# A drain of GpSimd behind the second last scatter of a sparse graph-attention kernel

## The chip, the cores and the metric

The kernel runs on one NeuronCore of a Trainium2 chip. The metric is device time in microseconds (us); the time shown is the median of three runs. Beside it stands one profiled execution, taken by the hardware profiler, from which all durations below come.

## The reference

One graph-attention layer over 3327 nodes with 1024 features, after a layer norm and a ReLU:

```python
h = jnp.maximum(_layernorm(x, axis=-1), 0.0)
f = h @ Wf + bf
g = h @ Wg + bg
e = jax.nn.relu(f @ g.T)
scores = jnp.where(adj > 0, e, NEG)          # NEG = -9e15
attention = jax.nn.softmax(scores, axis=1)
out = x + attention @ (h @ W + bW)
```

`adj` is symmetric with ones on its diagonal and holds about 0.5% ones, so that a node has some 10 to 40 neighbours.

## The kernel before

The kernel uses the sparsity. Its first part (up to about 265 us) normalises the rows into a table `hd` in device memory, multiplies Wf and Wg into one matrix, and turns the rows of `adj` into neighbour lists `pd`, sorted by degree. Its second part handles the nodes in 26 tiles of 128 (`NT` is 26). For each tile t it gathers neighbour rows of `hd` with indirect DMAs that GpSimd issues (`gather`, recorded at line 639), takes dot products with the tile's queries (VectorE, L1260), forms the softmax (ScalarE), adds up the weighted rows (VectorE L1313, ScalarE L1296 and TensorE L1300), and multiplies the sum by W (TensorE, L1328).

The end of a tile is a chain. `rc` scales the product from PSUM into a result buffer `xp`, of which there are two (`res`, used in turn): on ScalarE, L1339, for all tiles but the last, and on VectorE, L1337, with x added, for the last. For all tiles but the last `X` then gathers the tile's rows of x on top of `xp`, as an adding DMA (line 639). Last comes `scatter`, an indirect DMA of GpSimd that writes the 128 rows of `xp` to their places in `out` (L1346).

The order of work on each engine is written out by a planner in Python: `planned` simulates the steps with their durations and gives each a start, and the loop

```python
for start, (op, *at), held in plan:
    ...
    made[op](*at)
```

issues them in that order. The order on each engine is then fixed; semaphores do the rest. On GpSimd the last steps are the gather of x for tile 24 (`X`), the scatter of tile 24, and the scatter of tile 25, one after the other with nothing between.

After the loop all five engines load a flag, `bad` (L1372), that says whether the graph fits the assumptions of the sparse path. If it doesn't, a dense path runs (L1384, `with tc.If(bad > 0)`); with this input it doesn't run. On the side where it doesn't, GpSimd has waits on the semaphores of its DMAs and then one instruction, INC_SWDGE_SEM[...]. The program ends at the close of the tile context (L1409): each engine executes a DRAIN and they meet at a barrier, of which GpSimd is the leader. SyncE first passes through a row of waits on the semaphores of the program, among them the eight that INC_SWDGE_SEM raises. A second, short barrier follows.

Of the kernel before, what the change touches and what calls it, by code (L numbers as in the profile page):

```python
# [579 lines left out]
def edge_path(ctx: ExitStack, tc: tile.TileContext, x, adj, Wf, bf, Wg, bg, W, bW, out, flag):  # L580
# [11 lines left out]
    nc = tc.nc  # L592
# [7 lines left out]
    NT = (N + P - 1) // P  # L600
# [567 lines left out]
    with tc.manual_schedule(engines={  # L1168
# [175 lines left out]
        def scatter(t):  # L1344
            whole = ORDER[t] < N // P
            ins = nc.gpsimd.indirect_dma_start(  # L1346
                out=out[:, :],
                out_offset=bass.IndirectOffsetOnAxis(
                    ap=perm[:, ORDER[t] : ORDER[t] + 1] if whole else final, axis=0
                ),  # L1350
                in_=res[t % 2],
                in_offset=None,
                bounds_check=None if whole else N - 1,
                oob_is_err=whole,
            )
            tc.declare_no_dep(ins.ins, group="results", reason="other rows")
            tc.add_to_no_dep_group("results", ins.ins)

        def told(_):
            nc.vector.tensor_copy(flag[0:1, 0:1], ps_y[1][0:1, 0, 0:1])  # L1360

        made = {
            "fl": told, "L": L, "H": H, "x": fetch_x, "C": C, "F": F, "G": fetch, "M": M, "hT": turned, "hc": hc, "q": third, "qc": qc,
            "fq": fq, "d": dot, "S": greatest, "A": A, "E": E, "Y": Y, "T": T, "w": w, "p": p, "s": s, "fo": fo, "yt": yt,
            "yc": yc, "W": project, "rc": rc, "X": X, "O": scatter,
        }
        plan = sorted(planned(ROWS, PASSES, SEED, WIDE)[1], key=lambda step: step[0])
# [8 lines left out]
def kernel(tc: tile.TileContext, x, adj, Wf, bf, Wg, bg, W, bW, out):  # L1376

    nc = tc.nc  # L1380
    with tc.tile_pool(name="flag", bufs=1) as fpool:
        flag = fpool.tile([1, 1], I32, name="flag")
        bad = edge_path(tc, x, adj, Wf, bf, Wg, bg, W, bW, out, flag)
        with tc.If(bad > 0):  # L1384
            dense_path(tc, x, adj, Wf, bf, Wg, bg, W, bW, out)
# [27 lines left out]
```

## Time and profile before

| what | us |
|---|---|
| median of three runs (lowest, highest) | 1232.57 (1228.5, 1233.57) |
| the profiled execution's own time | 1233.38 |
| its span, first to last instruction | 1231.6 |
| what lies around the span | 1.8 |
| PE busy in the span | 1099.2 (89%) |
| DVE busy | 1120.3 (91%) |
| POOL (GpSimd) busy | 936.7 (76%) |
| ACT busy | 602.7 (49%) |
| start of the scatter of tile 24, and of tile 25 | 1208.89, 1219.76 |

PE is TensorE, DVE is VectorE, ACT is ScalarE, POOL is GpSimd, SP is SyncE; a name with a q behind it is the engine's sequencer, which executes semaphore, branch and drain instructions. These are not counted as busy time. An arrow to the left in a row stands between what is written and what is read or, behind an idle time, before what ended it. Start times count from the beginning of the span.

### The profile page before, as it was taken

Reading aid. Unit: us, or ns where it says so; the run is one execution under the profiler, and the core shown is the slowest. Engines: PE = TensorE matmul, PEld = TensorE weight load, DVE = VectorE, ACT = ScalarE, POOL = GpSimd, SP = SyncE. Lnnn points to the kernel's source line nnn. Section 1 sums busy time; section 2 is a strip of 40 time slices with the busy share of each in tenths; the row PEclk is TensorE's granted clock in tenths of the full one; section 3 lists DMA queues with packets and bytes.
Section 4 is the critical chain, followed back from the end, with each engine's and each line's share of the span. In section 5 each row is a group of like instructions: output and inputs, shape, how many; then the busy total and the mean of one; then the engine's idle time right before and its main releaser. Section 6 shows DMA issues by size and latency. Waiting matters only on the chain. (4 is left out here: it accounts for less than half of the span.)

```text
span 1231.6 us, 14006 instructions
## 1 busy us (share of the span) xinstructions
PE 1099.2 (89%) x4508; PEld 697.5 (57%) x4508; DVE 1120.3 (91%) x2192; ACT 602.7 (49%) x924; POOL 936.7 (76%) x677
## 2 busy tenths in 40 slices
PE   2799990799939899999999999999899999999995
PEld 2566660466627466556655666665465656556553
DVE  5999998758898999998999999999999999999991
ACT  6899986324617355436452455443343333434240
POOL 8999996177676888878878778777887888787821
PEclk9899995799979999999999999999999999999998
DMA  9999999589788999989899899888998999998942
GB/s 370 420 396 397 393 359 324 191 313 350 270 257 281 329 314 315 319 285 339 302 342 308 307 306 320 279 286 299 317 294 288 311 310 321 283 316 256 324 118 54
DMA packets 101913, 374.43 MB, mean 304 GB/s; under 512 B 14859, under 2 KB 18602, under 8 KB 98631
## 3 DMA queue, kind: packets, MB, share of 16 engines
q0 software_dynamic: 79584, 286.77, 69.4%
q1 hardware_dynamic: 22246, 86.68, 18.7%
q8 instruction: 37, 0.61, 0.2%
q14 instruction: 46, 0.38, 0.1%
HBM read 344.11 MB, written 29.30 MB: 303 GB/s over the span
## 5 line engine op out<-in xcount | busy, mean ns | idle before, releaser
L639 POOL DMA_INDIRECT G<-hd,ps x454 | 567.4, 1250 | 159.2 <-issue 107.0
L1260 DVE CUSTOM_DVE_ANT_0 junk<-G,q 128x1024 bf16<-128x1024 f32 x468 | 563.9, 1224 | 34.0 <-DMA G<-hd,ps 19.2
L1328 PE MATMUL p_o<-W_sb,yT 128*128 128x512 f32 x832 | 365.8, 593 | 4.7 <-issue 3.1
L1313 DVE SCALAR_TENSOR_TENSOR G<-G,sc 128x1024 f32<-128x1024 f32 (+1 forms) x281 | 354.5, 1262 | 6.8 <-ACT G L1285 3.7
L1247 PE MATMUL p_q<-A_sb,hT 128*128 128x342 f32 x1152 | 350.5, 455 | 7.8 <-ACT p_q L1256 5.7
L1247 PEld LDWEIGHTS p_q<-A_sb,hT 128*128 128x128 f32 x1152 | 214.7, 191 | 116.4 <-issue 12.7
L1328 PEld LDWEIGHTS p_o<-W_sb,yT 128*128 128x128 f32 x832 | 155.1, 189 | 189.0 <-issue 180.9
L1300 PE MATMUL p_y<-ident,G 128*128 128x128 f32 x1552 | 190.1, 275 | 12.7 <-DVE G L1313 6.8
L1300 PEld LDWEIGHTS p_y<-ident,G 128*128 128x128 f32 x1552 | 175.0, 142 | 40.8 <-issue 15.3
L704 POOL TENSOR_TENSOR r<-r,iotaj 128x1664 f32<-128x1664 f32 (+3 forms) x50 | 183.9, 3750 | 3.9 <-ACT r L697 3.9
L1296 ACT ACTIVATE G<-G,sc 128x1024 f32<-128x1024 f32 x168 | 179.2, 1138 | 0.1
L837 PE MATMUL ps_A<-WgT,WfT 128*128 128x342 f32 x432 | 130.5, 461 | 1.6 <-ACT WfT L832 1.6
L767 DVE MAX8 cand<-r 128x8 f32<-128x208 f32 (+2 forms) x416 | 118.9, 360 | 4.0 <-POOL r L704 3.7
L1339 ACT ACTIVATE xp<-p_o,rs 128x512 f32<-128x512 f32 x50 | 34.2, 685 | 172.7 <-PE p_o L1328 131.5
L837 PEld LDWEIGHTS ps_A<-WgT,WfT 128*128 128x128 f32 x432 | 81.7, 193 | 42.1 <-issue 2.3
L697 ACT ACTIVATE r<-r 128x3327 f32<-128x3327 int32 (+3 forms) x27 | 77.3, 2865 | 10.2 <-DMA r<-in_adj_dram 10.2
L1253 ACT COPY q<-p_q 128x342 f32<-128x342 f32 x72 | 31.6, 443 | 103.0 <-PE p_q L1247 59.5
L1324 ACT COPY yT<-p_y 128x512 f32<-128x512 f32 x52 | 30.0, 587 | 71.6 <-PE p_y L1300 59.6
L1243 ACT COPY hT<-p_t 128x512 f32<-128x512 f32 x48 | 27.4, 585 | 74.4 <-PE p_t L1240 37.9
L639 POOL DMA_INDIRECT xp<-in_x_dram,perm x25 | 44.3, 1772 | 21.1 <-ACT xp L1339 14.4
L1281 ACT ACTIVATE sc<-sc,nm 128x10 f32<-128x10 f32 (+10 forms) x36 | 10.9, 304 | 94.4 <-DVE nm L1271 66.2
L1346 POOL DMA_INDIRECT out_dram<-xp,perm x25 | 32.8, 1310 | 31.1 <-DMA xp<-in_x_dram,perm 22.9
(148 smaller groups left out, 728.4 us busy)
## 6 DMA issues: line engine op xcount, KB each, us to landing
r<-in_adj_dram SPq DMA_DIRECT2D x24, 1663.5 KB, 12.8
xt<-in_x_dram SPq DMA_DIRECT2D x22, 512.0 KB, 13.6
hd<-xt SPq DMA_DIRECT2D x22, 512.0 KB, 10.5
G<-hd,ps POOLq DMA_INDIRECT x454
A_sb<-in_L_gnn_Wg_dram SPq DMA_DIRECT2D x8, 512.0 KB, 18.4
A_sb<-in_L_gnn_Wf_dram SPq DMA_DIRECT2D x8, 512.0 KB, 12.0
W_sb<-in_L_gnn_W_dram SPq DMA_DIRECT2D x8, 512.0 KB, 7.4
cd<-cand SPq DMA_DIRECT2D x25, 64.0 KB, 12.6
```

The lines of the kernel that those rows point to most:

```text
L639: return nc.gpsimd.indirect_dma_start(out=to, out_offset=None, in_=table, in_offset=bass.IndirectOffsetOnAxis(ap=idx, axis=0), **kw,)
L697: nc.scalar.activation(r[:n, b:e], a[:n, b:e], AF.Sign, accum_out=to)
L704: eng.tensor_mul(r[:n, b:e], r[:n, b:e], iotaj[:n, b:e])
L767: nc.vector.max(cands[t][:n, s * 8 : s * 8 + 8], r[:n, s * SW : min(N, (s + 1) * SW)])
L837: nc.tensor.matmul(ps[:, :QB], WfTs[c][:, k, :], WgT[:, k, o : o + QB], start=(k == 0), stop=(k == KD - 1))
L1247: nc.tensor.matmul(ps_q[(3 * t + i) % 2][:, :QB], hT[:, k, :], A_sb[:, k, i * QB : (i + 1) * QB], start=False, stop=(k == KD - 1), skip_gr ...
L1260: nc.vector.tensor_tensor_reduce(junks[k % 2], row(t, k), q[:, :D], 1.0, 0.0, op0=ALU.mult, op1=ALU.add, accum_out=scs[t % 3][:, k : k + 1],)
L1296: nc.scalar.activation(g, g, AF.Copy, scale=scs[t % 3][:, k : k + 1])
L1300: nc.tensor.matmul(ps_y[g][:, c, :], of[:, (4 * g + c) * P : (4 * g + c + 1) * P], ident, is_transpose=True, start=((t, g) not in begun an ...
L1313: nc.vector.scalar_tensor_tensor(y, row_k, scs[t % 3][:, k : k + 1], y, op0=ALU.mult, op1=ALU.add)
L1328: nc.tensor.matmul(ps_o[o], yT[:, k, :], W_sb[:, k, o * CB : (o + 1) * CB], start=False, stop=(k == KD - 1), skip_group_check=True,)
L1339: nc.scalar.activation(to, ps_o[o], AF.Copy, scale=rss[t % 3])
```

## The change

Behind the scatter of tile 24, the second last that GpSimd issues, a drain of GpSimd is written:

```diff
             )
             tc.declare_no_dep(ins.ins, group="results", reason="other rows")
             tc.add_to_no_dep_group("results", ins.ins)
+            if t == NT - 2:
+                nc.gpsimd.drain()
```

In the built program GpSimd has one DRAIN more, which waits for no semaphore and raises none. It stands between the scatter of tile 24 and the setting of a register for the scatter of tile 25. The instructions of all engines and their waits are otherwise the same, in the same order. Later source lines move down by two (L1372, L1384 and L1409 become L1374, L1386 and L1411).

## Prediction

> **What bounds the kernel now.** VectorE (91%) and TensorE (89%) bound the middle; the change touches neither, so I went to the end. First view, the chain that ended last, its last pieces (start, us, what):
>
> ```profile
> 1204.69 14.02 PE p_o L1328 x32
> 1218.70 0.02 issue
> 1218.72 0.76 DVE xp L1337
> 1219.49 0.03 issue
> 1219.52 0.51 POOLq L1372
> 1220.03 0.75 POOL out_dram L1346
> ```
>
> The last product ends at 1218.7, VectorE takes 0.76, and GpSimd scatters. The chain stops at 1220.8, yet the span lasts to 1231.6: 10.8 us hold no busy engine and are not in this view. Second view, the timeline of GpSimd from 1200 on (start, us; idle before in brackets):
>
> ```profile
> 1201.95 1.56 POOL L639 DMA_INDIRECT xp<-in_x_dram,perm  x1 [11.01 <-ACT xp L1339]
> 1208.89 0.98 POOL L1346 DMA_INDIRECT out_dram<-xp,perm  x1 [5.39 <-DMA xp<-in_x_dram,perm]
> 1219.76 1.02 POOL L1346 DMA_INDIRECT out_dram<-xp,final  x1 [9.88 <-DVE xp L1337]
> ```
>
> Between its last two scatters GpSimd idles 9.88 us, waiting for VectorE. The new drain stands there. Third view, the sequencers' instructions by line (durations in ns: least, median, most; then first and last start). L1384 is the branch, L1409 the end, L1401 the start of the program:
>
> ```profile
> L1384 POOLq EVENT_SEMAPHORE  x5: 17/43/43, 1223.0 to 1223.6; - x5
> L1384 POOLq INC_SWDGE_SEM  x1: 1533/1533/1533, 1223.6 to 1223.6; - x1
> ...
> L1409 SPq EVENT_SEMAPHORE  x12: 27/28/28, 1225.1 to 1225.8; - x12
> L1409 SPq DRAIN  x2: 7/7/7, 1225.9 to 1225.9; - x2
> L1409 POOLq DRAIN  x1: 5503/5503/5503, 1225.2 to 1225.2; - x1
> ...
> L1409 POOLq DRAIN  x2: 46/74/103, 1230.9 to 1231.3; - x2
> ...
> L1401 POOLq INC_SWDGE_SEM  x1: 27/27/27, 0.2 to 0.2; - x1
> L1401 POOLq DRAIN  x1: 169/169/169, 0.4 to 0.4; - x1
> ```
>
> So the end is: the last scatter lands (GpSimd's last wait for DMA ends at 1223.6), INC_SWDGE_SEM 1.53 us, then a DRAIN of 5.50 us that all others wait for. The same two instructions took 0.03 and 0.17 us at the start, before GpSimd had issued a DMA; between the start and the end it issues 576. A drain right behind the long one takes 0.10. Fourth view, busy time by stretch (PE, PEld, DVE, ACT, POOL, clock, DMA share, GB/s):
>
> ```profile
> 1209.90:1219.50 9.60, 8.79 (x21) 3.58 (x19) 1.50 (x2) 0.00 (x0) 0.00 (x0) 1.00 0.15 59
> 1225.20:1230.70 5.50, 0.00 (x0) 0.00 (x0) 0.00 (x0) 0.00 (x0) 0.00 (x0) 0.50 0.00 0
> ```
>
> During the 5.50 us no engine works and no DMA moves a byte: the drain isn't waiting for data under way.
>
> **The drain that is added.** It costs GpSimd's sequencer a time D in the idle stretch. The trace has two rows for D: 0.05 to 0.17 us where no DMA of GpSimd went before, 5.50 where hundreds did. Hundreds did here (all but one of 576), so I take 5.5. It starts once the scatter of tile 24 is issued (1208.9 to 1209.9); if it also waits for that scatter to land, from about 1212.6 (the scatter's last semaphore count in the trace). It ends between 1208.9 + 5.5 = 1214.4 and 1212.6 + 5.5 = 1218.1. Queued behind it are a register move, a semaphore wait of 17 ns, the last scatter with the DMA it issues, and the load of the flag; the scatter waits for VectorE until 1219.5. Nobody else waits for anything behind the drain, and GpSimd has no gather left to issue. Hidden by the last product, with 1.4 to 5.1 us to spare: cost 0. Without that cover it would be the whole 5.5.
>
> **What it takes from the end.** [...]
>
> INC_SWDGE_SEM: at least 0.03 (the start's row, which is another use of it), at most 1.53. In the trace it posts its eight semaphores 8 to 9 ns apart, the first 1.42 us after it begins; [...] I take 0.2 us. Saved 1.53 - 0.20 = 1.33; ends: 0 to 1.50.
>
> The DRAIN: 5.50 becomes about 0.2 (between the rows of 0.10 and 0.17 and a little more for one DMA). What is late next is SyncE, not GpSimd: its first wait is released by INC_SWDGE_SEM's posts (1225.1), twelve waits and two drains take it to 1225.93, and the barrier then opens in about 0.05. Before, GpSimd was at the barrier at 1230.77, 5.59 after INC_SWDGE_SEM's end at 1225.18; after the change the barrier comes 0.80 after that end. Saved 5.59 - 0.80 = 4.79, not 5.3.
>
> Sum: 4.79 + 1.33 = 6.1 us. The profiled execution would go from 1233.38 to 1227.3, its span from 1231.6 to 1225.5. That execution was 0.8 above the median of the runs shown; taken off the median, 1232.57 - 6.1 = **1226.5 us**. The other edits (nothing else changes in the program) cost 0.
>
> [...] The row: nothing in flight, a drain of 5.50. [...] the row shows a drain that took 5.50 with GpSimd's last record over at 1220.8 and its DMA landed by 1223.6, so something besides being idle is waited for; I go by the row. [...] while INC_SWDGE_SEM stayed at 1.53: sum 1232.57 - 4.79 = 1227.8. [...]
>
> **The rivals.** (a) The price comes back: the 5.50 belongs to whatever stands right before the last drain (the last scatter, or INC_SWDGE_SEM itself), or the new drain is a matter of 0.1 us that clears nothing. Then the end keeps its 10.8 us: 1232.6. For it: one long drain is all there is in the trace, so a fixed price for each drain after a DMA fits as well. Against it: INC_SWDGE_SEM, 57 times longer than at the start, shows a second instruction that has grown, and the short last drains show that one drain clears it. (b) Only the drain shrinks: 1227.8, as above. (c) Slower: the new drain outlasts its cover. The last scatter starts later once the drain takes over 9.6 us from 1209.9 (7.0 if it begins at the landing, 1212.6). To be slower than before it must overrun by more than what the end saves, so D beyond 9.6 + 6.1 = 15.7 us, or beyond 9.6 if rival (a) holds too; over 0.5% slower then needs D = 15.8. It would take a drain of nearly three times the one row there is, in a stretch in which TensorE and the DMAs are at work (DMA share 0.15). At D = 17 with nothing saved: 1232.6 + 7.4 = 1240.
>
> **How the numbers follow.** The bound of 0.5%, about what a measurement of this kernel can tell from no change, is 6.16 us, so 1226.4. Chances: [...] 0.82 (its own range: 1226.1 with INC_SWDGE_SEM at 0, and about 3 us either way for runs, whose three times spread over 5.1); (b) 0.04; (a) 0.10; (c) 0.04. The likeliest case stands almost on the bound: 6.1 against 6.16. What I have left uncounted goes one way ([...] the branch and the two short drains after the barrier come sooner or shorter), so I give two thirds of it, 0.55, to faster by over 0.5%, and 0.27 to within. Faster 0.55; within 0.27 + 0.04 + 0.10 = 0.41; slower 0.04. The range, 1222.5 to 1231.0, holds the likeliest case but for its edges (0.05) and all of (b), and leaves out (a) and (c): 0.81.
>
> **What the profile of the changed kernel would show.** A DRAIN of GpSimd at the scatter's line between 1209 and 1218, of about 5.5 us; the start of the last scatter still 0.3 behind VectorE's last record, at about 1219.8; INC_SWDGE_SEM at 0.2 to 0.3; the first drain of the end under 0.3; SyncE's drain, not GpSimd's, last before the barrier; some 4.7 us from the end of the last scatter to the end of the span in place of 10.8. The prediction is wrong if the last drain is still 5 us long (rival a), if INC_SWDGE_SEM keeps 1.5 (rival b), or if the last scatter's idle time is ended by GpSimd itself (rival c).

## The result, and the profile after

The changed kernel takes 1226.6 us (median of 22 runs, 1220.87 to 1233.30), the kernel before 1232.08 (median of 22 runs, 1221.88 to 1237.24). The ratio is 0.9959, with a 95% interval of 0.9942 to 0.9976: 0.4% faster, between 3.0 and 7.1 us. The profiled execution took 1224.52 us, with a span of 1222.7.

The end of the span is where to look. The sequencers' instructions by line, of the changed kernel (durations in ns: least, median, most; then first and last start). L1359 is the new drain, L1386 the branch and L1411 the end of the program, up to the barrier:

```profile
L1359 POOLq DRAIN  x1: 6652/6652/6652, 1205.8 to 1205.8; - x1
...
L1386 POOLq INC_SWDGE_SEM  x1: 203/203/203, 1220.9 to 1220.9; - x1
...
L1411 SPq EVENT_SEMAPHORE  x12: 27/28/28, 1221.1 to 1221.7; - x12
L1411 SPq DRAIN  x2: 7/7/7, 1221.8 to 1221.9; - x2
L1411 POOLq EVENT_SEMAPHORE  x2: 17/17/17, 1221.9 to 1222.0; - x2
L1411 POOLq DRAIN  x1: 140/140/140, 1221.2 to 1221.2; - x1
```

INC_SWDGE_SEM went from 1533 to 203 ns and the first drain of the end from 5503 to 140. GpSimd's drain is over at 1221.3; SyncE's second drain at 1221.9 is now the last before the barrier. The timeline of GpSimd, of the changed kernel:

```profile
1199.31 1.56 POOL L639 DMA_INDIRECT xp<-in_x_dram,perm  x1 [10.94 <-ACT xp L1339]
1206.06 0.99 POOL L1346 DMA_INDIRECT out_dram<-xp,perm  x1 [5.18 <-DMA xp<-in_x_dram,perm]
1217.12 1.02 POOL L1346 DMA_INDIRECT out_dram<-xp,final  x1 [10.08 <-DVE xp L1337]
```

The last scatter's wait is still ended by VectorE. The drain begins in the sequencer 0.24 us before the scatter of tile 24, whose issue is over at 1207.04, and goes on until 1212.47. What follows it on GpSimd, by line:

```profile
L1346 POOLq MOVE  x1: 29/29/29, 1212.5 to 1212.5; - x1
L1346 POOLq EVENT_SEMAPHORE  x1: 17/17/17, 1212.6 to 1212.6; - x1
L1346 POOL DMA_INDIRECT out_dram<-xp,final x1: 1017/1017/1017, 1217.1 to 1217.1; - x1
```

From the drain's end to VectorE's result at 1216.84 there are 4.4 us to spare. From the start of the last scatter to the end of the span it was 11.81 us before (1219.756 to 1231.562) and is 5.58 (1217.120 to 1222.695): 6.23 us less. The two profiled spans differ by 8.9; the other 2.6 us lie ahead of the last scatter, where the kernels are the same, and are within what runs of one kernel differ by (1220.87 to 1233.30 for the changed one).

### The profile page after: what moved, and what is told of

It is laid out like the page before. It is cut to its first block, busy times and chain, and to the rows that moved or that the text cites. A ratio compares the mean times of both kernels' runs of the same rounds, so it can differ in the third digit from the quotient of the medians.

```text
span 1222.7 us, 14007 instructions
## 1 busy us (share of the span) xinstructions
PE 1099.3 (90%) x4508; PEld 696.8 (57%) x4508; DVE 1121.7 (92%) x2192; ACT 601.9 (49%) x924; POOL 942.3 (77%) x677
## 5 line engine op out<-in xcount | busy, mean ns | idle before, releaser
L639 POOL DMA_INDIRECT G<-hd,ps x454 | 577.4, 1272 | 153.9 <-issue 98.2
L1240 PE MATMUL p_t<-ident,G 128*128 128x128 f32 x192 | 30.1, 286 | 27.9 <-DMA G<-hd,perm 27.7
```

The costliest lines, as they stand in the source:

```text
L639: return nc.gpsimd.indirect_dma_start(out=to, out_offset=None, in_=table, in_offset=bass.IndirectOffsetOnAxis(ap=idx, axis=0), **kw,)
```

## The experiments

They ran in two sets, each on one chip. The kernel before took 1242.54 us in the first (23 runs; the drains behind tiles 12, 16, 19 and 25) and 1240.18 in the second (31 runs; the others); times are compared within a set, and kernels that ran once are read for their traces alone. Two readings of the 5.50 us were to be told apart. In the first, which the expectations call the records theory, the last drain and INC_SWDGE_SEM take longer the more DMAs GpSimd has issued since the drain before; a "record" is one DMA's share of that time and nothing more. In the second only the first long drain of a run is long: wherever the new drain stands ahead of the last scatter, the first drain of the end then takes 0.14 us and INC_SWDGE_SEM 0.20, as in the changed kernel. All edits move one line, the condition of the new drain.

**One drain earlier, so that some DMAs come after it.** Four runs:

```diff
-            if t == NT - 2:
+            if t == 12:        # 176 DMAs after it; t == 16: 98; t == 19: 39; t == 21: 12
                 nc.gpsimd.drain()
```

> The drain stands behind the scatter of tile 12 alone; GpSimd issues 176 DMAs after it. Records theory [...]: the first drain of the end is long again, 1.7 us if each DMA adds the same (5.5 / 576 = 9.6 ns), 5.5 us if the number of records has a limit below 176; INC_SWDGE_SEM grows with it, to 0.6 or 1.5 us. [...] The drain in the stream takes 5.4 us and up in either.

> The drain stands behind the scatter of tile 16 alone; 98 DMAs follow. Records theory: the first drain of the end takes 0.9 us if all 576 count alike, or up to 5.5 if there is a limit under 98; between them if the limit is between 98 and 176. INC_SWDGE_SEM between 0.4 and 1.5. [...]

> The drain stands behind the scatter of tile 19 alone; 39 DMAs follow. Records theory: the first drain of the end stands to that of the run with 98 as 39 to 98, if no limit is met: 0.4 us if all 576 count alike, 2.2 at most. INC_SWDGE_SEM 0.3 to 0.8. [...]

> The drain stands behind the scatter of tile 21 alone; 12 DMAs follow. By the 82 ns for each record that the runs with 39 and 98 give, the first drain of the end takes 1.0 us, and by 20 ns for each INC_SWDGE_SEM takes 0.4. A price that is fixed from some number on, or has a step, would show as 3 us or as 0.1.

The first drain of the end, by line, in the runs with 176, 98, 39 and 12 DMAs after the new drain, and behind each INC_SWDGE_SEM of the same run:

```profile
L1411 POOLq DRAIN  x1: 5979/5979/5979, 1253.1 to 1253.1; - x1
...
L1386 POOLq INC_SWDGE_SEM  x1: 1650/1650/1650, 1251.4 to 1251.4; - x1
```

```profile
L1411 POOLq DRAIN  x1: 8062/8062/8062, 1246.5 to 1246.5; - x1
...
L1386 POOLq INC_SWDGE_SEM  x1: 2160/2160/2160, 1244.3 to 1244.3; - x1
```

```profile
L1411 POOLq DRAIN  x1: 3243/3243/3243, 1238.5 to 1238.5; - x1
...
L1386 POOLq INC_SWDGE_SEM  x1: 980/980/980, 1237.5 to 1237.5; - x1
```

```profile
L1411 POOLq DRAIN  x1: 1038/1038/1038, 1231.1 to 1231.1; - x1
...
L1386 POOLq INC_SWDGE_SEM  x1: 440/440/440, 1230.6 to 1230.6; - x1
```

The second reading falls: each of these is a later drain, and three of the four took 3.2 to 8.1 us. From 12 to 39 to 98 DMAs the drain grows by (3243 - 1038) / 27 = 81.7 and (8062 - 3243) / 59 = 81.7 ns for each, INC_SWDGE_SEM by (980 - 440) / 27 = 20.0 and (2160 - 980) / 59 = 20.0. So in these runs a drain costs 58 ns and 81.7 for each DMA since the drain before, INC_SWDGE_SEM 200 and 20. The last drain of the changed kernel, with one DMA left, fits (140 ns); its INC_SWDGE_SEM, at 203, lies 17 under the line. It isn't the bytes that count: 2 of the last 39 DMAs and 5 of the last 98 fetch neighbour lists, with rows of 100 bytes against the 4096 of `hd`, and the two slopes agree only if these count as much as the others. All these DMAs have 128 rows, so whether the price goes by the DMA or by its rows stays open.

The sizes were not as expected: 5.5 us was taken for the most that the last drain can cost, and 98 DMAs gave 8.1 us, 39 gave 3.2 where 2.2 was the most allowed; that these two stand as 39 to 98 held. The run with 176 breaks the row: 5979 ns after 176 DMAs are less than 8062 after 98. At the prices above both instructions are worth the same number of DMAs there, (5979 - 58) / 81.7 = 72.5 and (1650 - 200) / 20 = 72.5, and for the kernel before, with 576, (5503 - 58) / 81.7 = 66.6 and (1533 - 200) / 20 = 66.7. So after 176 and 576 DMAs a part of them costs nothing at the end, where 98 were paid in full. What decides how many are paid was not shown.

Each of these kernels ran once; in the same order they took 1261.66, 1257.14, 1244.44 and 1234.67 us (the last in the second set).

**The drain without its cover.** Behind the last scatter instead of the second last:

```diff
-            if t == NT - 2:
+            if t == NT - 1:
                 nc.gpsimd.drain()
```

> The drain stands behind the last scatter instead of the second last: the same drain without its cover. From the last scatter's start: 1.0 for its issue, 5.4 of clearing (its landing, some 3.8 after its start, lies within), then the load of the flag and the branch, 2.75 from the branch to GpSimd's next instruction, which lay beside the landing before, 0.6 of waits, INC_SWDGE_SEM 0.2, SyncE's row of waits 0.8, the rest 0.9: 12.0 us from the last scatter's start to the end of the span, against 11.8 before and 5.6 with the change. Time as before, 1232. If the clearing itself were not the price (the rival that only something right before the last drain is long), the end would hold a second long drain and be 5.5 longer than before.

Measured: 1242.65 against 1242.54 us, ratio 1.0001 (0.9972 to 1.0030), and 1240.1 - 1228.07 = 12.0 us from the last scatter's start to the end of the span. The timeline of GpSimd, and its sequencer by line:

```profile
1228.07 1.02 POOL L1346 DMA_INDIRECT out_dram<-xp,final  x1 [10.23 <-DVE xp L1337]
```

```profile
L1359 POOLq DRAIN  x1: 6762/6762/6762, 1227.8 to 1227.8; - x1
...
L1386 POOLq INC_SWDGE_SEM  x1: 189/189/189, 1238.4 to 1238.4; - x1
...
L1411 POOLq DRAIN  x1: 56/56/56, 1238.6 to 1238.6; - x1
```

From the end of the scatter's issue (1229.08) the drain goes on to 1234.59, 5.51 us, where the last drain of the kernel before took 5.50. The drain at the end, with no DMA since, takes 56 ns, against the 58 of the line. The same drain with the same saving behind it gives no gain in this place. Before, the load of the flag and the branch lay beside the scatter's landing (the branch at 1220.1, the last wait for a DMA over at 1223.6); here they come after the drain (the branch at 1235.2), inside which the landing lies: the DMAs moved 176 GB/s from 1229 to 1232 and nothing from 1232 to 1234.6. The gain of the change is its place.

**A second drain in the stream of gathers**, beside the change itself:

```diff
-            if t == NT - 2:
+            if t in (12, NT - 2):
                 nc.gpsimd.drain()
```

> Drains behind the scatters of tile 12 and of tile 24. The end as in the changed kernel: first drain of the end 0.14 us, INC_SWDGE_SEM 0.20. The drain behind tile 24 has 175 DMAs behind the first one: by the records theory with a limit (73 records were left after 176) 5.9 us after its scatter's issue, hidden. The first drain holds GpSimd for some 8 us in the stream of gathers; in the run with tile 12 alone VectorE then waited 8.9 us for gathers. If that is all lost, the time is 8 to 9 us over the changed kernel and 2 to 4 over the kernel before; if the buffers win some of it back, between. [...]

> The changed kernel beside the others on this chip: 5 to 6 us under the kernel before; INC_SWDGE_SEM 0.20 and first drain of the end 0.14 us; the drain in the idle stretch some 5.4 us from the end of its scatter's issue.

The change took 1234.16 us, ratio 0.9972 (0.9948 to 0.9997), or 3.5 us less (0.4 to 6.4) where 5 to 6 were expected; with two drains it was 1245.66, ratio 1.0010 (0.9978 to 1.0043), both against the same kernel before. The end was as expected: INC_SWDGE_SEM 203 ns in both, the first drain of the end 140 ns with the change alone and 135 with two. GpSimd's sequencer and its timeline around the drain behind tile 12, and what VectorE waited for from 900 to 920, in the run with two:

```profile
L1359 POOLq DRAIN  x2: 7123/8630/10137, 901.8 to 1228.3; - x2
...
902.05 1.82 POOL L1346 DMA_INDIRECT out_dram<-xp,perm  x1 [1.77 <-DMA xp<-in_x_dram,perm]
912.72 0.96 POOL L639 DMA_INDIRECT G<-hd,ps  x1 [8.85 <-issue]
```

```profile
DVE junk L1260 <- DMA G<-hd,ps: 6.8, 1, 6.8
```

GpSimd issues nothing for 8.85 us and the buffers filled ahead do not cover it: VectorE, which is 90% busy over the span, waits 6.8 us for a gather. In the stretch from 860 to 960 it waited 8.0 us in all for gathers; in the same stretch of the change alone the list of waits shows none for a gather. With the second drain no gain over the kernel before is left to see. Its price is not settled more closely: the medians are 11.5 us apart, the ratios some 4.7, and the intervals of the ratios overlap. The drain behind tile 24 went on for 5.90 us after its scatter's issue (1229.50 to 1235.40), worth 71.5 DMAs at the price above, with 175 issued since the first drain; after 176 it was 72.5. This too is a long drain behind a long one. In the run with the drain behind tile 21 GpSimd stood still for 7.41 us with gathers still to issue, and VectorE waited for none of them from 1165 to 1215: the buffers filled ahead seem to have been enough there.

## Why the prediction was right

**The end is what the change touches: right.** 11.81 us became 5.58.

**The drain that is added: right in its cover, lucky in its size.** I took 5.5 us for D from one row. The row of the new drain is 6.65 long, because it begins 0.24 us before the scatter ahead of it, whose issue takes 0.99; counted from the end of that issue it is 5.43, which is 58 + 65.7 x 81.7 ns, 0.07 less than the last drain took before. The landing of tile 24's scatter, 3.5 us after its start, lies inside and shows no price of its own: behind the last scatter, too, it was 5.51 from the issue's end with the landing inside, against 5.50 at the end before, where all had landed. It was luck that the length there was that of the end: the drain behind tile 12 went on for 8.1 us after its scatter's issue. That too would have been hidden, up to 1215.1, with 1.7 us to spare. The 0.05 us that I gave beside 0.17 for a drain with no DMA before it stands at the end, behind the long drain; it is a row for a drain with no DMA since the one before. The new drain ended 5.43 after the issue, at the early end of what I allowed, and 4.4 us ahead of VectorE's result (1.4 to 5.1 predicted).

**INC_SWDGE_SEM: right.** 1.53 to 0.20, saved 1.33 as in the sum.

**The last drain, and who is late next: right.** From INC_SWDGE_SEM's end to the barrier it was 5.59 us and is 1221.90 - 1221.12 = 0.78; saved 4.81, predicted 4.79. GpSimd's drain alone shrank by 5.36; SyncE's twelve waits keep 0.55 of that.

**The sum: right.** 1.33 + 4.81 is 6.14; with 0.09 less from the last scatter's start to INC_SWDGE_SEM it makes the 6.23 of the traces, and the runs' interval, 3.0 to 7.1 us, holds it. That 1226.5 and the measured 1226.6 lie 0.1 apart is luck: the three runs that I started from have a median 0.5 above that of the 22, and the medians differ by 5.5, not 6.1. The case to which I gave 0.82, that both instructions shrink, is what was seen. The time with INC_SWDGE_SEM at 0 comes to 1226.25 by the sum, not to 1226.1. What I left uncounted did go the way I thought, but is 0.09 us and not enough to lean on: with a gain of 0.4%, and an interval of 0.24 to 0.58%, the runs don't say that the bound of 0.5% was passed, and their middle lies under it. The 0.55 that I gave to the far side was too much; half and half was all that the sum supported.

**That a drain takes the time away: right in the main, wrong in one part.** I expected the last drain and INC_SWDGE_SEM to fall to what one DMA costs. That they grow with the DMAs since the drain before is shown by the runs with 12, 39 and 98 DMAs after it (1.04, 3.24 and 8.06 us for the drain, 0.44, 0.98 and 2.16 for INC_SWDGE_SEM), and that a drain takes the time away by the 0.14 us behind the new drain. That each DMA of the whole run adds to it is wrong: after 576 the drain took 5.50 us, after 98 it took 8.06. So the 5.5 us had no tie to the 576; with another number of DMAs it could have been the 8.1 of the run with 98. What the chip does in this time was not shown.

**The rivals.** That the price comes back (a) is refuted by the 140 ns in the trace, and by the 56 ns right behind INC_SWDGE_SEM where the drain stood behind the last scatter; rival (b) by INC_SWDGE_SEM's 203. Rival (c), a drain that outlasts its cover, didn't happen behind tile 24; behind tile 12 the drain did outlast what the buffers cover, and the wait fell on VectorE.

## What to carry to other kernels

Where a program ends in a long drain of GpSimd, ask whether it pays there for DMAs that GpSimd has issued, though they have landed, as this one did (5.50 us from 1225.2 on, with the last wait for a DMA over at 1223.6, and 0.14 with the drain ahead of it); look for it behind the last row of the chain, in time that no engine's busy share shows. It can then be paid earlier, in a stretch where GpSimd waits for something else for longer than that drain takes (in these runs 82 ns for each of up to 98 DMAs since the last one; 8.1 us was the most read here) and where the critical path does not go through GpSimd's issue. In the stream of gathers that feeds VectorE (6.8 us of waiting there), and behind the last DMA (ratio 1.0001), the same line won nothing.

## What the runs showed that I had not expected

The price of a DMA is the same in both sets: the run with 12 DMAs, of the second, lies on the line of those with 39 and 98, of the first (81.7 ns each way). With one DMA after the new drain or none, the first drain of the end keeps within 5 ns of that line (140, 135 and 56 ns against 139.7, 139.7 and 58), and INC_SWDGE_SEM lies 11 to 17 ns under (203 against 220, 189 against 200).

The length of the last drain is not monotone in the DMAs since the drain before: after 12, 39 and 98 it is worth 12, 39 and 98 DMAs, but after 176 it is worth 72.5 and after 576 66.6. The first drains in the stream, counted from the end of the issue ahead of them and read at the same price, are worth 98 DMAs after 400 (tile 12, in both runs), about 80 after 564 (tile 21) and 66 after 575 (the change). DMAs were under way while these drains ran (a share of 0.16 from 903.9 to 912 in the run with two), and how much of a reading is a wait for them was not shown. None of these is over 98.

The first instruction of GpSimd behind the branch at L1386 starts 2.7 us after the branch's end (1217.52 to 1220.21). In the kernel before and the changed one this lies beside the last scatter's landing (3.5 to 3.7 us after its start in the changed one); in the run with the drain behind the last scatter it is exposed, from 1235.28 to 1237.92.
